# Loading gamma and the value bias inside the first slot, and changing the filters and pointwise weights earlier in it

## The chip, the cores and the metric

The kernel runs on one core of one Trainium2 chip. The metric is the device time of one execution in microseconds (us). A core has five instruction streams that run beside each other and wait for each other through semaphores. TensorE (PE in the profile) multiplies matrices; PEld is its loading of weights. VectorE (DVE) and ScalarE (ACT) do elementwise work, GpSimd (POOL) does elementwise work and issues transfers, and SyncE (SP) only issues transfers. Transfers run on 16 DMA engines. Each stream takes its instructions strictly in the order in which the program wrote them.

## The reference

Two layers act on an array x of 4 pictures of 64 by 64 pixels with 256 channels.

Layer 0 is full self-attention in each picture (4096 tokens, queries and keys of 32 channels), scaled by one number gamma and added to x:

```
q = x @ Wq + bq;  k = x @ Wk + bk;  v = x @ Wv + bv
attn = softmax(q k^T)                       # 4096 x 4096 per picture
x = gamma * (attn @ v) + x
```

Layer 1 filters each channel with three 3x3 filters ("perceived", 768 channels), applies two pointwise layers with an exact gelu between them and adds the result to x, and then adds a 3x3 windowed attention of the result:

```
perceived = depthwise_conv3x3(x, w_perc) + b_perc      # 256 -> 768
hid = gelu(perceived @ w_up1 + b_up1)                  # 768 -> 512
h = x + hid @ w_up2 + b_up2                            # 512 -> 256
out = h + local_attention_3x3(h, w_qkv, b_qkv)
```

Everything is float32.

## The kernel before, in words

Tokens are cut into blocks of 512 (eight rows of a picture). There are 8 blocks in each of 4 pictures, so 32 *slots*; a slot does the attention of the 512 queries of one block over the 4096 keys of its picture. A slot runs through 16 *points* (`for point in range(points)`, L1176). At each point the program writes the two score matmuls `energy` for weights that are needed two points later (L374; the exponential on ACT, L383, follows), then eight matmuls `product` of weights with values into the accumulators (L392), then one addition on DVE of the weights to the running denominator (`add_up`, L421, its addition at L433). In the slots from the second on, some points run in a split form (L414, L430, L435). The work of layer 1 on earlier blocks is put between the points as jobs. The exponentials go through a ring of three buffers `p` (L382), the scores through a single buffer `e` (L376), and keys through a ring of two tiles `ka` (L293), each loaded by four transfers from a packed copy in device memory (L219 to L223).

The first slot is special. The queries, keys and values of the first picture are projected during it: a start-up part writes blocks 0 to 2 (L1091 to L1106), and then at each odd point two further projections follow (`early_jobs`, L1121; written at L1246). At the even points SP issues the loads of the keys that are due two pairs of points later (`load_keys`, L1182).

All order is that of the written program: the function runs under a manual schedule, so each engine's stream is the sequence in which the Python code calls it, and semaphores for true dependences are put in by the framework.

What the change touches:

- L1107 to L1112, after the start-up part and ahead of the first slot: `gam` (gamma copied to all 128 partitions) and `gbv` (the value bias, two numbers per partition) are loaded by SP, and DVE makes gbv times gamma and `gam_parts`, gamma times a constant. Both are read first when a slot is finished (`finish`, L495 and L501).
- L1218 to L1224, at the end of point 1 of the first slot: GpSimd issues the loads of the layer-1 filters `wb`, their bias, the 1.5 MB of pointwise weights `wup1`, and its bias.
- L1225 to L1230: at points 5, 6 and 7, DVE runs `clear_tap` (L642), 20 very small instructions each, which recombine the filters so that some taps become zero. At point 5 a copy of the bias stands ahead of it.
- L1231 to L1232: at points 9 to 14, DVE runs `turn_weights` (L674), four instructions each on 512 columns, which apply the same recombination to `wup1`.
- After point 15 DVE sums the denominator across partitions (`partial_sums`, L450, lines L458 and L459), PE folds the partial sums (L477), and DVE scales the result into x (`finish`). The first use of the changed filters and weights is in the third slot (`perceive`) and the fourth (`hidden_part`); in the second slot GpSimd reads the changed `wup1` (L1238 and L1240).

Of the kernel before, what the change touches and what calls it, by code (L numbers as in the profile page):

```python
# [12 lines left out]
ALU = mybir.AluOpType  # L13
# [3 lines left out]
P = 128  # L17
# [16 lines left out]
MULT = 3  # L34
# [5 lines left out]
NG = NT // GRP  # L40
# [9 lines left out]
SPLIT = 4096.0  # L50
# [8 lines left out]
def attention_then_perception_kernel(  # L59
# [19 lines left out]
    nc = tc.nc  # L79
# [17 lines left out]
    def unshifted():  # L97
# [1006 lines left out]
            project_v(2, i)  # L1104
        fetch(4)
        fetch(5)  # L1106
        gam = loaded(gamma.partition_broadcast(P), "gam", [P, 1])  # L1107

        gbv = loaded(b_v.rearrange("o (c p) -> p (o c)", p=P), "gbv")
        nc.vector.tensor_scalar(gbv, gbv, gam[:, 0:1], None, ALU.mult)  # L1110
        gam_parts = pool.tile([P, 1], F32, tag="gam_parts", name="gam_parts")
        nc.vector.tensor_scalar(gam_parts, gam, 1.0 + 1.0 / SPLIT, None, ALU.mult)  # L1112
        wlv = pool.tile([P, CH, C], F32, tag="wlv", name="wlv")
        combine = combine_steps()

# [8 lines left out]
        for slot in range(NSLOT):  # L1124
            b, g = divmod(slot, NBLK)
            if slot >= RING:
                renew(slot)
            k, a = slot - LAG_HID, slot - LAG_ATT

            jobs = [  # L1130
                job(hidden_part, k, 0, 0) + job(local_values, k - 1, 1),
                job(local_denominator, a) + job(hidden_part, k, 0, 1),
                job(hidden_part, k, 1, 0), job(hidden_part, k, 1, 1),
                job(local_product, a, 0), job(local_product, a, 1),
                job(update, k, 0), job(update, k, 1), job(guide, k, 0),
                job(guide, k, 1), job(local_values, k, 0), job(scores, k, 0),
                job(scores, k, 1) + job(local_sum, k - 1), [], job(border, k), [],
            ]
            if slot in (1, 2):
                jobs[0] = [lambda: next(combine)] * 2  # L1140
            nxt = []
            if g == NBLK - 1 and b + 1 < B:
                nxt = [projections(slot + 1 + i) for i in range(NBLK)]
                for i in range(2):
                    fetch(slot + 1 + i)
            if slot == 0:
                nxt = [early_jobs[2 * i : 2 * i + 2] for i in range(NG)]
            conv = perceive(slot - LAG_PERC, mixed) if slot >= LAG_PERC else iter(())
            n_mixed = sum(tap != 0 for _, tap, *_ in mixed)
            n_steps, stepped = n_mixed, 0  # L1150


            share = [2, 4, 8, 6, 4, 1, 7, 3, 6, 3, 4, 2, 2, 1, 1, 0]
            if slot == NSLOT - 1:

                jobs = [
                    job(hidden_part, k, 0, 0) + job(local_values, k - 1, 1),
                    job(local_denominator, a) + job(hidden_part, k, 0, 1),  # L1160
                    job(hidden_part, k, 1, 0), job(hidden_part, k, 1, 1) + job(local_product, a, 0),
                    job(update, k, 0), job(update, k, 1) + job(local_product, a, 1),
                    job(guide, k, 0) + job(local_values, k, 0),
                    job(guide, k, 1) + job(local_values, k, 1),
                    job(scores, k, 0) + job(hidden_part, k + 1, 0, 0),
                    job(scores, k, 1) + job(local_sum, k - 1) + job(hidden_part, k + 1, 0, 1),
                    job(hidden_part, k + 1, 1, 0) + job(local_total, a + 1)
                    + job(local_reciprocal, a + 1),
                    job(hidden_part, k + 1, 1, 1), job(update, k + 1, 0) + job(border, k),
                    job(local_product, a + 1, 0) + job(update, k + 1, 1),  # L1170
                    job(local_product, a + 1, 1) + job(local_values, k + 1, 0),
                    job(local_values, k + 1, 1),
                ]
                conv = chain(conv, perceive(slot - 1, upper))
                n_steps += sum(tap != 0 for _, tap, *_ in upper)
            for point in range(points):  # L1176
                G, half = divmod(point, 2)
                after = slot + (G + 1) // NG, (G + 1) % NG
                if half == 0:
                    ahead = slot + (G + 2) // NG, (G + 2) % NG  # L1180
                    if ahead[0] < NSLOT:
                        load_keys(*ahead)  # L1182
                    if 0 < ahead[0] < NSLOT:
                        load_values(*ahead)
                    if G == NG // 2 and slot + 1 < NSLOT:
                        spread_queries(slot + 1)
                behind = slot + (point + 1) // points, *divmod((point + 1) % points, 2)
                if in_parts(*behind):
                    high_part(*behind)
                if after[0] < NSLOT:  # L1190
                    energy(*after, half)
                soon = slot + (point + 3) // points, *divmod((point + 3) % points, 2)
                if in_parts(*soon):
                    load_forms(*soon)
                for do in jobs[point]:
                    do()
                if slot == NSLOT - 1 and point == NHC + 2 * RING:
                    nc.sync.dma_start(out=wup1[:, :MULT, C:], in_=turned_up)
                product(slot, G, half)

                if point == 0:
                    add_up(slot, 0, 0)
                if point < points - 1:
                    add_up(slot, *divmod(point + 1, 2))
                else:
                    partial_sums(slot)


                if slot < NSLOT - 1:
                    to = sum(share[: point + 1])  # L1210
                else:
                    to = min(n_steps, -(-(point + 1) * n_steps // (points - 2)))
                    if point < 3:
                        to = min(to, n_mixed // MULT)
                while stepped < to:
                    next(conv, None)
                    stepped += 1
                if slot == 0 and point == 1:  # L1218
                    wb = const.tile([P, CH, MULT, TAPS + 1], F32, tag="wb", name="wb")
                    nc.gpsimd.dma_start(out=wb[:, :, :, :TAPS], in_=w_perc)  # L1220
                    bias = loaded(b_perc, "bperc", queue=nc.gpsimd)
                    wperc, bperc = wb[:, :, :, :TAPS], wb[:, :, :, TAPS]
                    wup1 = loaded(w_up1, "wup1", queue=nc.gpsimd)
                    bup1 = loaded(b_up1, "bup1", queue=nc.gpsimd)  # L1224
                if slot == 0 and NG - MULT <= point < NG:  # L1225
                    if point == NG - MULT:
                        scratch = tile_of([P, NB], "rden", "scratch")
                        scratch = scratch[:, : (TAPS + 3) * CH].rearrange("p (j c) -> p j c", c=CH)
                        nc.vector.tensor_copy(bperc, bias)
                    clear_tap(point - NG + MULT)  # L1230
                if slot == 0 and NG < point <= NG + 2 * MULT:  # L1231
                    turn_weights(*divmod(point - NG - 1, 2))  # L1232
                if slot == 0 and point == NG:

                    next(combine)
                    blqk = loaded(b_lqk, "blqk", queue=nc.gpsimd)
                if slot == 1 and point == NG:
                    nc.gpsimd.dma_start(out=turned_up, in_=wup1[:, :MULT, C:])  # L1238
                    wup2 = loaded(w_up2, "wup2", queue=nc.gpsimd)
                    mix_weights(  # L1240
                        *blocks_of(wup1, MULT, C), *(wmix[:, i] for i in range(3))
                    )
                    bup2 = loaded(b_up2, "bup2", queue=nc.gpsimd)
                    nc.gpsimd.dma_start(out=wlv, in_=w_qkv[:, :, 2 * C :])
                    blv = loaded(b_lv.partition_broadcast(P), "blv", [P, C], queue=nc.gpsimd)
                if nxt and half == 1:  # L1246
                    for do in nxt[G]:
                        do()
                    if slot and G + 2 < NBLK:
                        fetch(slot + 1 + G + 2)  # L1250
            for _ in conv:
                pass
            if slot < NSLOT - 1:
                next(finish(slot))
# [466 lines left out]
```

## Time and profile before

| what | value |
|---|---|
| median of 3 runs | 3305.59 us (3302.0 to 3307.45) |
| the profiled execution's own time | 3305.77 us |
| span from its first to its last instruction | 3304.1 us |
| PE busy | 3264.6 us, 99% |
| DVE busy | 2905.2 us, 88% |
| ACT busy | 1349.2 us, 41% |
| POOL busy | 500.7 us, 15% |
| mean granted PE clock | 0.997 |

Busy times are those in which an instruction of the engine is under way. The profile's lines give a start in us from the first instruction, a length, the engine (a q behind it means the sequencer that issues), the line of the kernel, the operation and the names of tiles (out<-in), and in brackets how long the engine sat idle before it and what ended that. A transfer's "time to landing" runs from its issue to its last semaphore update.

### The profile page before, as it was taken

The numbers are of one execution on the slowest core, as the hardware profiler recorded it, in microseconds if no ns is written. First come the engines' busy times: TensorE is split into PE (matmuls) and PEld (weight loads), VectorE is DVE, ScalarE is ACT, GpSimd is POOL, SyncE is SP. The second block draws the span as 40 slices with busy tenths as digits, with TensorE's granted clock in tenths as the row PEclk, the third lists the DMA queues.
The fourth block names the chain that finished last, engine by engine and source line by source line (L and its number), as shares of the span: only waits on it lengthen the run. The fifth ranks groups of instructions, "written<-read, shape, count | busy, mean of one in ns | idle before, by whom it ended". The sixth has DMA issues, their size and how long they took to land.

```text
span 3304.1 us, 35658 instructions
## 1 busy us (share of the span) xinstructions
PE 3264.6 (99%) x11986; PEld 2170.4 (66%) x11986; DVE 2905.2 (88%) x4243; ACT 1349.2 (41%) x1647; POOL 500.7 (15%) x627
## 2 busy tenths in 40 slices
PE   8999999999999999999999999999999999999998
PEld 5556666666666666676666666666666666666655
DVE  4788899888999999987999999998799999999894
ACT  3334444444444444444444444444444444444331
POOL 2200011120111110112001111101210011111121
PEclk9999999999999999999999999999999999999999
DMA  6533333464333433346333333435643333333100
GB/s 207 184 113 108 115 115 117 143 193 139 117 115 122 128 116 114 117 149 209 117 116 117 115 122 121 128 105 174 200 130 103 121 112 115 122 122 121 48 18 27
DMA packets 246910, 410.90 MB, mean 124 GB/s; under 512 B 92272, under 2 KB 93312, under 8 KB 246592
## 3 DMA queue, kind: packets, MB, share of 16 engines
q1 hardware_dynamic: 231632, 370.15, 36.8%
q0 software_dynamic: 7408, 24.95, 1.9%
q10 hardware_dynamic: 7680, 13.44, 1.1%
q8 instruction: 99, 1.62, 0.2%
q14 instruction: 91, 0.75, 0.1%
HBM read 346.92 MB, written 60.69 MB: 123 GB/s over the span
## 4 chain that ended last, share of the span: by engine, by line
PE 92%; DVE 4%; DMA 1%; ACT 1%; issue 1%; SPq 0%; POOL 0%; ACTq 0%; DVEq 0%; POOLq 0%
PE acc L402 30%; PE acc L414 16%; PE e L378 7%; PE dx L762 6%; PE hid_bc L705 5%; PE hid_gf L705 5%; PE hid_de L705 5%; PE lv L925 3%; PE g L858 3%; PE v L325 3%; PE lo L1059 3%; PE s L966 2%; PE hid_a L705 2%; DVE perc L592 2%; PE qk L259 1%; PE hid L737 1%
## 5 line engine op out<-in xcount | busy, mean ns | idle before, releaser
L402 PE MATMUL acc<-p,v 128*128 128x512 f32 x2472 | 1113.5, 593 | 0.2 <-ACT v L339 0.2
L592 DVE SCALAR_TENSOR_TENSOR perc<-xp,wb,perc 128x526 f32<-128x526 f32 (+1 forms) x1356 | 969.1, 773 | 0.1
L383 ACT ACTIVATE p<-e 128x1024 f32<-128x1024 f32 x512 | 524.3, 1024 | 1054.3 <-PE e L378 888.0
L402 PEld LDWEIGHTS acc<-p,v 128*128 128x128 f32 x2472 | 466.8, 190 | 486.8 <-issue 472.5
L433 DVE TENSOR_TENSOR den<-den,p 128x1024 f32<-128x1024 f32 x448 | 564.9, 1261 | 1.0 <-ACT p L383 0.6
L991 POOL TENSOR_TENSOR lp<-lp,near 128x396 f32<-128x396 f32 x60 | 150.8, 2513 | 1965.3 <-ACT lp L986 1965.3
L378 PE MATMUL e<-qa,ka 128*128 128x512 f32 x1024 | 427.9, 499 | 13.0 <-ACT p L383 13.0
L378 PEld LDWEIGHTS e<-qa,ka 128*128 128x128 f32 x1024 | 190.0, 190 | 162.7 <-issue 128.0
L388 ACT ACTIVATE ph<-p 128x1024 fp32r<-128x1024 f32 x203 | 214.4, 1056 | 199.4 <-PE acc L414 130.5
L414 PE MATMUL acc<-ph,v 128*128 128x512 f32 x812 | 264.4, 447 | 0.0
L430 DVE TENSOR_TENSOR pl<-p,ph 128x1024 fp32r<-128x1024 f32 x203 | 253.2, 1247 | 12.1 <-ACT ph L388 12.0
L435 DVE SCALAR_TENSOR_TENSOR pg<-pl,ph 128x1024 fp32r<-128x1024 f32 x203 | 256.7, 1264 | 0.0
L762 PE MATMUL dx<-hid,wup 128*128 128x512 f32 x512 | 229.8, 592 | 0.0
L414 PE MATMUL acc<-pg,vf 128*128 128x512 f32 x812 | 222.0, 395 | 1.1 <-DVE pg L435 1.1
L414 PE MATMUL acc<-pl,vf 128*128 128x512 f32 x812 | 219.6, 392 | 0.0
L414 PEld LDWEIGHTS acc<-ph,v 128*128 128x128 f32 x812 | 148.3, 189 | 51.0 <-issue 26.8
L414 PEld LDWEIGHTS acc<-pg,vf 128*128 128x128 f32 x812 | 152.5, 188 | 37.0 <-DVE pg L435 1.5
L414 PEld LDWEIGHTS acc<-pl,vf 128*128 128x128 f32 x812 | 152.7, 188 | 35.6 <-DVE pl L430 0.4
L598 DVE TENSOR_TENSOR perc<-perc 128x262 f32<-128x262 f32 x360 | 168.0, 481 | 6.3
L1014 POOL TENSOR_TENSOR lsum<-lsum,lp 128x99 f32<-128x99 f32 (+1 forms) x179 | 171.8, 966 | 11.7
L728 ACT ACTIVATE hid<-hid,bup 128x512 f32<-128x512 f32 x120 | 80.1, 715 | 215.8 <-DVE hid L712 215.8
L762 PEld LDWEIGHTS dx<-hid,wup 128*128 128x128 f32 x512 | 96.8, 190 | 98.6 <-issue 93.4
(203 smaller groups left out, 3872.4 us busy)
## 6 DMA issues: line engine op xcount, KB each, us to landing
vf<-packed_f SPq DMA_DIRECT2D x203, 512.0 KB, 4.1
ka<-packed SPq DMA_DIRECT2D x1016, 64.0 KB, 3.0
v<-packed_f SPq DMA_DIRECT2D x203, 256.0 KB, 2.7
v<-packed_v SPq DMA_DIRECT2D x203, 256.0 KB, 2.9
v<-packed_v SPq DMA_DIRECT2D x45, 512.0 KB, 3.5
xp<-in_x SPq DMA_DIRECT2D x30, 528.0 KB, 6.8
xc<-in_x SPq DMA_DIRECT2D x56, 256.0 KB, 3.8
out<-lo SPq DMA_DIRECT2D x56, 256.0 KB, 2.0
```

The source lines that it names most:

```text
L378: nc.tensor.matmul(e[:, i, :], lhsT=keys[s, G][:, bass.ts(2 * half + i, P)].bitcast(F32R), rhs=queries[s].bitcast(F32R), start=True, stop= ...
L383: nc.scalar.activation(p, e, AF.Exp)
L388: nc.scalar.activation(high.bitcast(F32R), weights[s, G, half], AF.Identity, scale=BELOW)
L402: nc.tensor.matmul(accs[s][c], lhsT=v[:, i, bass.ts(c, P)], rhs=p[:, i, :], start=(first and i == 0), stop=(last and i == 1),)
L414: nc.tensor.matmul(accs[s][to + c], lhsT=w[:, i, bass.ts(c, P)].bitcast(F32R), rhs=x[:, i, :].bitcast(F32R), start=(to > 0 and n == 0 and ...
L430: nc.vector.tensor_tensor(low.bitcast(F32R), p, high, ALU.subtract)
L433: nc.vector.tensor_tensor(den, before, p, ALU.add)
L435: nc.vector.scalar_tensor_tensor(gap.bitcast(F32R), low, -SPLIT, high, ALU.mult, ALU.add)
L592: nc.vector.scalar_tensor_tensor(acc, win, wt, acc, ALU.mult, ALU.add)
L705: nc.tensor.matmul(ps[:, n * C : (n + 1) * C], lhsT=w(j), rhs=rows_of(mixes[s, j][:, kind, :]), start=(j == 0), stop=(j == MULT - 1),)
L762: nc.tensor.matmul(ps, lhsT=wup2[:, d, bass.ts(c, P)], rhs=hids[s][:, d, :], start=(d == 0), stop=(d == NHC - 1),)
L1014: nc.gpsimd.tensor_tensor(to, to, near_ws[block, half][:, t_, of, :], ALU.add)
```

## The change

The two loads of gamma and the value bias move from before the first slot to the end of its point 1, behind GpSimd's loads of the layer-1 weights in the text, and stay on SP. Their two DVE instructions move to point 3, ahead of the first `clear_tap`. The three `clear_tap` calls move from points 5, 6, 7 to points 3, 4, 5. The six `turn_weights` calls move from points 9 to 14 to points 6 to 11, so two and three points sooner. No instruction is added or removed.

```diff
@@ -1104,12 +1104,7 @@
             project_v(2, i)
         fetch(4)
         fetch(5)
-        gam = loaded(gamma.partition_broadcast(P), "gam", [P, 1])
-
-        gbv = loaded(b_v.rearrange("o (c p) -> p (o c)", p=P), "gbv")
-        nc.vector.tensor_scalar(gbv, gbv, gam[:, 0:1], None, ALU.mult)
         gam_parts = pool.tile([P, 1], F32, tag="gam_parts", name="gam_parts")
-        nc.vector.tensor_scalar(gam_parts, gam, 1.0 + 1.0 / SPLIT, None, ALU.mult)
         wlv = pool.tile([P, CH, C], F32, tag="wlv", name="wlv")
         combine = combine_steps()
 
@@ -1222,14 +1217,18 @@
                     wperc, bperc = wb[:, :, :, :TAPS], wb[:, :, :, TAPS]
                     wup1 = loaded(w_up1, "wup1", queue=nc.gpsimd)
                     bup1 = loaded(b_up1, "bup1", queue=nc.gpsimd)
-                if slot == 0 and NG - MULT <= point < NG:
-                    if point == NG - MULT:
+                    gam = loaded(gamma.partition_broadcast(P), "gam", [P, 1])
+                    gbv = loaded(b_v.rearrange("o (c p) -> p (o c)", p=P), "gbv")
+                if slot == 0 and MULT <= point < 2 * MULT:
+                    if point == MULT:
+                        nc.vector.tensor_scalar(gbv, gbv, gam[:, 0:1], None, ALU.mult)
+                        nc.vector.tensor_scalar(gam_parts, gam, 1.0 + 1.0 / SPLIT, None, ALU.mult)
                         scratch = tile_of([P, NB], "rden", "scratch")
                         scratch = scratch[:, : (TAPS + 3) * CH].rearrange("p (j c) -> p j c", c=CH)
                         nc.vector.tensor_copy(bperc, bias)
-                    clear_tap(point - NG + MULT)
-                if slot == 0 and NG < point <= NG + 2 * MULT:
-                    turn_weights(*divmod(point - NG - 1, 2))
+                    clear_tap(point - MULT)
+                if slot == 0 and 2 * MULT <= point < 4 * MULT:
+                    turn_weights(*divmod(point - 2 * MULT, 2))
                 if slot == 0 and point == NG:
 
                     next(combine)
```

## The prediction

> **What bounds the kernel now.** I read the page first. PE is busy for 99% of the span and leads the chain, so the change can only move time where PE stands still; and only the first slot is edited. So I read that slot in the timeline, then the waits around each hole of PE, then the transfers behind the first hole. PE has two holes there. In the chain that ended last, start and length in us:
>
> ```profile
> 26.76 2.68 SPq L85
> 29.48 9.74 DMA gbv<-in_b_v
> 39.60 1.14 DVE den L433
> 40.82 1.03 ACT p L383
> 41.90 1.22 PE e L378 x2
> ```
>
> The value bias is issued at 29.48 and lands at 39.2. DVE, in order, stands before its scaling; the first denominator addition is behind it. That addition frees the oldest `p` buffer, ACT's fourth exponential waits for the buffer, and PE waits for that exponential, because it frees the only `e`. The timeline has the same from each engine's side:
>
> ```profile
> 39.31 0.23 DVE L1110 TENSOR_SCALAR gbv<-gbv,gam 128x2 f32<-128x2 f32 x1 [12.78 <-DMA gbv<-in_b_v]
> 40.82 1.02 ACT L383 ACTIVATE p<-e 128x1024 f32<-128x1024 f32 x1 [14.28 <-DVE den L433]
> 41.90 1.22 PE L378 MATMUL e<-qa,ka 128*128 128x512 f32 x2 [8.02 <-ACT p L383]
> ```
>
> PE idles 8.02 us, from 33.88 to 41.90. It also restarts slowly. Stages of the timeline, with PE, PEld, DVE, ACT and POOL busy and then PE's granted clock:
>
> ```profile
> 33.90:41.90 8.00, 0.00 (x1) 0.01 (x1) 2.48 (x4) 1.08 (x2) 0.00 (x0) 0.78 0.48 171
> 41.90:45.30 3.40, 3.40 (x5) 1.83 (x6) 2.32 (x4) 2.12 (x3) 0.00 (x0) 0.51 0.41 145
> 82.60:118.20 35.60, 35.35 (x108) 19.92 (x106) 28.72 (x40) 12.74 (x18) 4.84 (x9) 1.00 0.54 183
> ```
>
> The third row shows the rest of the slot: PE without holes, DVE 81% full. The second hole is at the slot's end. The last `turn_weights` stands ahead of DVE's transpose, and PE's fold waits:
>
> ```profile
> 115.75 3.11 DVE L679 SCALAR_TENSOR_TENSOR wup<-wup,coef 128x512 f32<-128x512 f32 x4
> 118.77 0.70 DVE L458 STREAM_TRANSPOSE turned<-den 128x512 f32<-128x512 f32 x1
> 120.34 0.58 PE L477 MATMUL dps<-parts,fold 128*128 128x16 f32 x2 [2.16 <-DVE parts L459]
> ```
>
> The first hole has a second cause behind the first: the keys of the very matmul that restarts. Issues in narrow windows, KB each and us to landing:
>
> ```profile
> wup<-in_w_up POOLq DMA_DIRECT2D x1, 1536.0 KB, 9.6
> gam<-in_gamma SPq DMA_DIRECT2D x1, 0.5 KB, 11.4
> gbv<-in_b_v SPq DMA_DIRECT2D x1, 1.0 KB, 9.7
> ka<-packed SPq DMA_DIRECT2D x1, 64.0 KB, 9.3
> ka<-packed SPq DMA_DIRECT2D x2, 64.0 KB, 8.6
> ```
>
> The last of the four key transfers is issued at 31.5 and lands at 39.9, only 2.0 us before PE restarts. So taking away the wait for gbv alone would give 2.0 us and not 8.0; the rest depends on how much earlier the keys land.
>
> **What the Trainium skill says.** "DMA: Bandwidth & Descriptors", Queues, rings and completion order: each DMA engine goes round the queues that have work for it, packet by packet, and consumes one ring in order. The trace agrees: gamma's 512 bytes, issued at 26.76, land at 38.1, when GpSimd's 1.5 MB (29.28 to 38.8) are nearly through; the bias and the keys follow in the order of their issue. Same page, Issuing engines are not separate DMA queues: the queues share 16 engines; the window 26.5 to 33.9 has them 100% busy. "TensorE: Matmul & The Clock Gate", What's actually happening: an idle window of about 3.4 us halves the clock, a busy one restores it. Here the clock is about a half for 6.8 us, some 38.4 to 45.2, 3.3 us of it after the restart.
>
> **The change, part by part.**
>
> *The two loads leave their place.* SP issues gam in 2.68 us (26.76 to 29.44) and gbv in 0.50. The four key transfers (30.08 to 31.97) inherit that place and are issued about 3.2 us sooner, from 26.8. Gam's long issue is not its own, I assume: SP was similarly slow (2.24 us) at one of the picture loads before it. So the last key may be issued at 28.7 at best and 31.0 at worst; neither decides, since the ring ahead holds picture loads that land until 32.6. What decides is how fast a transfer directly behind them gets through beside `wup1`. Gamma did just that in the before trace: 128 rows, 8 per DMA engine, landing at 38.1. The keys are 128 rows too, but of 2 KB. Estimate: 38.1, plus 8 rows x 84 ns (a 2 KB packet's length in this trace) = 0.7, gives **38.8**. Lower bound: four small transfers that slip between the weights could land with the filter bias, on GpSimd's queue at 34.3, plus some of the 1.5 MB; about 36.5. Upper bound: they come out only behind the weights, as now: 39.9, less the bias's own rows, 39.6. I take 38.8.
>
> *DVE no longer waits.* It is free at 26.5; the additions run at 26.6 and 27.8 (1.22 us each); ACT's fourth exponential runs as soon as PE has its scores, at 28.6. Both are done before PE finishes the projection at 33.88. PE then needs only the keys and starts at 38.9 instead of 41.9: **3.0 us**. If the keys come at 36.5 or 39.6 it is 5.3 or 2.2.
>
> *Clock.* The idle stretch 35 to 38.4 still halves the clock up to 41.8. Before, 3.3 us after the restart ran at half speed and cost 1.65; now (41.8 - 38.9)/2 = 1.45: **0.2 us**. If PE restarts early enough, by some 36.7, the window may count as busy and the whole 1.65 come back.
>
> *The loads' new place on SP.* At point 1 they stand after these keys and before the packed queries of blocks 4 and 5, four picture loads and the keys of point 2. They delay those by their issue, 1 to 3 us. The packed store waits for DVE's L272 after the projection, about 35.3, so the issue is hidden; the keys of point 2 would be issued near 42 instead of 47.5 and PE wants them near 51.5. If that cover were gone, each us would cost one.
>
> *The scaling at point 3.* Two DVE instructions, 0.23 + 0.15 us, on a DVE that in the before trace is idle from 46.2 to 57.2. Gbv lands behind the keys near 40; DVE comes there near 43: no wait. Queued behind it are the filter change, the split of value block 3, and the additions of points 4 and on. The addition at point 4 is first wanted by the exponential at point 6, near 64.5. From gbv to the end of that addition DVE needs 3.7 + 1.8 + 1.2 us, so gbv could land as late as 57 before PE pays.
>
> *The filter change two points sooner.* Three times 3.7 us (61.43 to 65.1 for the first), the first in the idle stretch, at no cost. The other two come with the additions at points 4 and 5: from 55.6 DVE works 1.2 + 3.7 + 1.2 + 3.7 to 65.4, so L272 of the next queries, ready at 62.9, waits 2.5 us. Only a key load behind it waits, landing near 72 for a matmul at 74.5. The filters landed at 34.2, the bias at 34.3. Cost: zero; without that cover up to 2.5.
>
> *The weight change three points sooner.* Six times 3.1 us at points 6 to 11. With two additions and one value split a pair of points asks 2.4 + 6.2 + 1.8 = 10.4 us of DVE while PE needs 11.25; the before trace ran points 9 to 14 so and PE had no hole. `wup1` landed at 38.8. Cost: zero.
>
> *The slot's end.* Nothing stands between the last addition and the transpose. L458 follows L440 at 115.75 and the partial sums are ready at 117.15, before PE's last product ends at 118.18. The 2.16 us hole goes: **2.16 us**. Then DVE's chain from the fold to L435, 15 us long, leads as before, so PE's slightly better clock there gains nothing (1.10 us of waiting for L435 stay or grow).
>
> *Sum.* 3.0 + 0.2 + 2.16 = 5.4 us. From the profiled execution's 3305.77 (span 3304.1 and 1.7 around it): **3300.4 us**. The median of the runs is 3305.59, 0.2 below the profiled one. Afterwards PE leads without a break, so the gain should reach the end.
>
> **Rivals.**
>
> *The keys stop being a limit.* They get through by about 36.5, or 35. Then 5.4 to 7 us of the hole go, with all or part of the 1.65 of clock, and the end's 2.16: 8 to 11 us, about **3296.5**. For it: 256 KB is little, and the small filter loads passed in 5.6 to 6.3 us. Against it: gamma, in just this place, needed 11.4.
>
> *The keys stay the limit, or the end's hole returns elsewhere.* Keys at 39.6, 2.2 us, with the end giving 0 to 2: 1 to 4 us, **3303**. For it: before, everything on SP's queue came out behind the 1.5 MB. Against the second half: nothing else is due on DVE there.
>
> *Slower: the scaling stalls DVE at point 3.* Gamma and the bias have the longest landing times on SP and now stand behind the keys. To lose, gbv has to land after 57; each us beyond costs one, and a net loss over 6.6 us needs some 57 + 5.4 + 6.6 = 69, 39 us after its issue, against 9.7 now. **3313**. Against it: GpSimd's load ends near 39.
>
> **How the numbers follow.** A measurement of this kernel can tell about 0.2%, 6.6 us; so the forecast is inside that. Forecast (gain 4 to 7, 3299 to 3302): 0.52, of which 0.10 lies beyond 6.6 us with the scatter of runs (3302.0 to 3307.45). First rival 0.26, second 0.18, slower 0.04. Faster 0.26 + 0.10 = 0.36; same 0.42 + 0.18 = 0.60; slower 0.04. The range 3295.5 to 3304.3 leaves out the far ends of the first two rivals and the third.
>
> **What would show it.** Right: PE idle about 5 us before the L378 of point 2, now ended by a transfer of ka landing near 38.8 and not by ACT; first L433 at 26.6; no idle time before L1110's successor beyond what DVE has anyway; L477 without a wait on DVE. Wrong: keys landing before 37 or after 39.7; a wait on gbv that reaches PE; new holes of PE at points 4 to 11, or a hole at L477 that remains.

## The result, and the profile after

| | before | after |
|---|---|---|
| median of 13 runs | 3306.24 us (3301.24 to 3309.28) | 3299.50 us (3295.54 to 3302.27) |
| the profiled execution's own time | 3305.77 us | 3302.27 us |
| its span | 3304.1 us | 3300.5 us |
| PE restarts at point 2 of the first slot | 41.90 | 39.09 |
| the fold at the first slot's end (L477) | 120.34 | 115.24 |
| the first product with `pg` in the second slot (L414), called the milestone below | 135.55 | 130.18 |

The ratio of the runs is 0.998, 95% interval 0.9972 to 0.9989: 6.7 us faster, and the interval allows 3.6 to 9.3 (the two ends of the ratio times 3306.24). The forecast was 3300.4. Below, a run's own time is that of its profiled execution.

The chain that ended last, of the kernel after (start, length, what); these four lines stand where the chain of before had the bias, an addition and an exponential:

```profile
28.52 1.25 SPq L223
30.81 8.08 DMA ka<-packed
39.09 1.07 PE e L378 x2
40.17 4.72 PE acc L402 x8
```

The same in its timeline, with the second hole's place below:

```profile
26.36 1.22 DVE L433 TENSOR_TENSOR den<-p,p 128x1024 f32<-128x1024 f32 x1
39.09 1.07 PE L378 MATMUL e<-qa,ka 128*128 128x512 f32 x2 [4.26 <-DMA ka<-packed]
42.40 0.22 DVE L1224 TENSOR_SCALAR gbv<-gbv,gam 128x2 f32<-128x2 f32 x1
112.38 0.69 DVE L440 TENSOR_TENSOR den<-den 128x512 f32<-128x512 f32 x1
113.18 0.71 DVE L458 STREAM_TRANSPOSE turned<-den 128x512 f32<-128x512 f32 x1
115.24 0.29 PE L477 MATMUL dps<-parts,fold 128*128 128x16 f32 x2
126.28 0.73 PE L378 MATMUL e<-qa,ka 128*128 128x512 f32 x2 [1.98 <-ACT p L383]
```

DVE now begins its additions at 26.36 and not at 39.5. PE still stops at point 2, but what ends the stop is the transfer of the keys. The bias is scaled at 42.40 with no wait in front. At the slot's end the transpose follows the last addition and the fold waits for nobody. The last line is new in size: the second slot's third pair of score matmuls waited 0.56 us before and 1.98 now:

```profile
131.65 0.74 PE L378 MATMUL e<-qa,ka 128*128 128x512 f32 x2 [0.56 <-ACT p L383]
```

This line is from the kernel before. DVE's chain from the fold leads there in both kernels. PE ran at half clock from 120.3 to 123.7 in the kernel before and runs at full clock after the fold now, so it only comes to the wait sooner.

Stages of the kernel after (PE, PEld, DVE, ACT, POOL busy, then PE's clock, DMA share, GB/s):

```profile
33.90:39.10 5.20, 0.94 (x3) 0.09 (x2) 1.83 (x2) 1.26 (x2) 0.00 (x0) 1.00 0.93 292
39.10:42.70 3.60, 3.60 (x6) 1.87 (x7) 1.44 (x5) 1.02 (x1) 0.00 (x0) 0.53 1.18 254
54.00:74.70 20.70, 20.70 (x67) 11.25 (x66) 18.92 (x56) 7.05 (x10) 1.62 (x3) 1.00 0.36 123
2363.70:2367.10 3.40, 3.40 (x5) 1.35 (x4) 3.23 (x7) 0.90 (x1) 0.12 (x1) 0.50 0.73 217
```

The first row is the hole, with the DMA engines 93% busy; the second the restart at half clock. The third holds the filter changes and the first weight changes at their new points: DVE is busy for 18.9 of 20.7 us and PE has no hole. The fourth explains why this one execution shows only 3.5 us at its end. At the milestone it is 5.37 us ahead; near 2365 it loses 1.8 us, 1.7 of them in a window at half clock, which the profiled execution before did not have there:

```profile
2364.00:2370.00 6.00, 3.19 (x12) 1.82 (x11) 2.88 (x5) 2.76 (x4) 1.86 (x3) 1.00 0.53 188
```

That line is from the kernel before. PE stands still there for 2.8 us before and 2.7 after, waiting for an exponential; a halved clock follows in some of the profiled executions and not in others. So the experiments are read at the milestone, to some tenths of a us, and the end times give the total.

### The profile page after: what moved, and what is told of

It reads as the page before. It is cut to its first block, busy times and chain, and to the rows that moved or that the text cites. A ratio compares the mean times of both kernels' runs of the same rounds, so it can differ in the third digit from the quotient of the medians.

```text
span 3300.5 us, 35656 instructions
## 1 busy us (share of the span) xinstructions
PE 3266.1 (99%) x11986; PEld 2170.0 (66%) x11986; DVE 2905.6 (88%) x4243; ACT 1349.2 (41%) x1647; POOL 501.6 (15%) x627
## 4 chain that ended last, share of the span: by engine, by line
PE 85%; DVE 12%; issue 2%; DMA 1%; ACT 1%; POOL 0%; SPq 0%; ACTq 0%; DVEq 0%; POOLq 0%
PE acc L402 28%; PE acc L414 14%; PE e L378 6%; PE dx L762 5%; PE hid_bc L705 5%; DVE perc L592 5%; PE hid_gf L705 4%; PE hid_de L705 4%; PE v L325 3%; PE lv L925 3%; PE g L858 3%; PE lo L1059 2%; PE hid_a L705 2%; PE s L966 2%; DVE den L433 2%
## 5 line engine op out<-in xcount | busy, mean ns | idle before, releaser
L433 DVE TENSOR_TENSOR den<-den,p 128x1024 f32<-128x1024 f32 x448 | 565.2, 1262 | 4.1 <-ACT p L383 3.9
L414 PE MATMUL acc<-ph,v 128*128 128x512 f32 x812 | 264.4, 447 | 0.0
L430 DVE TENSOR_TENSOR pl<-p,ph 128x1024 fp32r<-128x1024 f32 x203 | 253.3, 1248 | 12.1 <-ACT ph L388 12.0
L435 DVE SCALAR_TENSOR_TENSOR pg<-pl,ph 128x1024 fp32r<-128x1024 f32 x203 | 256.9, 1265 | 0.0
L414 PE MATMUL acc<-pg,vf 128*128 128x512 f32 x812 | 222.0, 395 | 1.1 <-DVE pg L435 1.1
L414 PE MATMUL acc<-pl,vf 128*128 128x512 f32 x812 | 219.7, 392 | 0.0
L414 PEld LDWEIGHTS acc<-ph,v 128*128 128x128 f32 x812 | 148.3, 189 | 51.1 <-issue 26.8
L414 PEld LDWEIGHTS acc<-pg,vf 128*128 128x128 f32 x812 | 152.4, 188 | 37.0 <-DVE pg L435 1.5
L414 PEld LDWEIGHTS acc<-pl,vf 128*128 128x128 f32 x812 | 152.7, 188 | 35.6 <-DVE pl L430 0.4
```

The costliest lines, as they stand in the source:

```text
L414: nc.tensor.matmul(accs[s][to + c], lhsT=w[:, i, bass.ts(c, P)].bitcast(F32R), rhs=x[:, i, :].bitcast(F32R), start=(to > 0 and n == 0 and ...
L430: nc.vector.tensor_tensor(low.bitcast(F32R), p, high, ALU.subtract)
L433: nc.vector.tensor_tensor(den, before, p, ALU.add)
L435: nc.vector.scalar_tensor_tensor(gap.bitcast(F32R), low, -SPLIT, high, ALU.mult, ALU.add)
```

## The experiments

**The two halves of the change, each alone.** The first keeps the loads' and the scaling's new place, and puts filter and weight changes back (against the kernel after; `...` marks lines left out):

```diff
-                if slot == 0 and MULT <= point < 2 * MULT:
-                    if point == MULT:
+                if slot == 0 and point == MULT:
                         ... the two scaling instructions
+                if slot == 0 and NG - MULT <= point < NG:
+                    if point == NG - MULT:
                         ...
-                    clear_tap(point - MULT)
-                if slot == 0 and 2 * MULT <= point < 4 * MULT:
-                    turn_weights(*divmod(point - 2 * MULT, 2))
+                    clear_tap(point - NG + MULT)
+                if slot == 0 and NG < point <= NG + 2 * MULT:
+                    turn_weights(*divmod(point - NG - 1, 2))
```

> Only the two loads and their two scaling instructions are moved; filter and weight changes stay at points 5 to 7 and 9 to 14. Theory A (two separate holes: the first ends with the keys' landing, the second is the last weight change standing before the transpose): PE restarts at about 39.1, the fold at L477 keeps its wait of 2.2 us, and the first L414 on pg in the second slot (135.55 before, 130.18 after) starts at 132.7. Rival C (the earlier filter changes are what frees DVE): PE restarts at 41.9 and the first L414 on pg stays at 135.5.

Its timeline:

```profile
39.29 1.19 PE L378 MATMUL e<-qa,ka 128*128 128x512 f32 x2 [4.80 <-DMA ka<-packed]
118.50 0.37 PE L477 MATMUL dps<-parts,fold 128*128 128x16 f32 x2 [2.18 <-DVE parts L459]
```

The first hole is shortened as in the kernel after, the second is as before. The milestone came at 133.50 and not 132.7, because of the clock:

```profile
37.40:44.25 6.85, 4.96 (x7) 2.49 (x8) 1.67 (x4) 1.02 (x1) 0.00 (x0) 0.50 1.07 260
```

Here 5.0 us after the restart ran at half speed, (44.25 - 39.29)/2 = 2.5 us lost, against 3.4/2 = 1.7 in the kernel after, whose halved window lay at 39.2 to 42.64. Own time 3303.44. The filter changes do not free DVE; the loads do.

The second half alone is the same exchange of point numbers in the kernel before, with the loads left in place:

```diff
-                if slot == 0 and NG - MULT <= point < NG:
-                    if point == NG - MULT:
+                if slot == 0 and MULT <= point < 2 * MULT:
+                    if point == MULT:
                         ...
-                    clear_tap(point - NG + MULT)
-                if slot == 0 and NG < point <= NG + 2 * MULT:
-                    turn_weights(*divmod(point - NG - 1, 2))
+                    clear_tap(point - MULT)
+                if slot == 0 and 2 * MULT <= point < 4 * MULT:
+                    turn_weights(*divmod(point - 2 * MULT, 2))
```

> The loads and the scaling stay before the first slot; filter and weight changes move to points 3 to 5 and 6 to 11. Theory A: PE restarts at 41.9 as before, no wait at L477, the first L414 on pg starts at 133.0 (2.2 to 2.6 sooner than 135.55). Rival C: the restart comes forward to 39; a third possibility, that the earlier changes crowd DVE: a new hole of PE between 55 and 80 and the first L414 on pg at 135 or later.

```profile
41.76 1.22 PE L378 MATMUL e<-qa,ka 128*128 128x512 f32 x2 [7.96 <-ACT p L383]
118.13 0.29 PE L477 MATMUL dps<-parts,fold 128*128 128x16 f32 x2
```

The first hole is untouched, the wait at the fold is gone, and the milestone is at 133.06, 2.49 us sooner. No new hole of PE in the slot. Own time 3302.11. With 2.05 for the loads alone (135.55 - 133.50) the two halves make 4.5 of the 5.37; the rest is the 0.8 us of clock just named.

**Which of the changes fills the second hole.** In the kernel after, only `turn_weights` goes back to points 9 to 14:

```diff
-                if slot == 0 and 2 * MULT <= point < 4 * MULT:
-                    turn_weights(*divmod(point - 2 * MULT, 2))
+                if slot == 0 and NG < point <= NG + 2 * MULT:
+                    turn_weights(*divmod(point - NG - 1, 2))
```

> The changed kernel with the weight changes back at points 9 to 14, the filter changes staying at points 3 to 5. If the last weight change is the whole second hole: restart 39.1, the wait of 2.2 us at L477 is back, the first L414 on pg starts at 132.7, as in the run with the loads alone, so the filter changes' new place is worth nothing. If the filter changes had a part in it, the wait at L477 is under 2 us.

```profile
38.96 1.19 PE L378 MATMUL e<-qa,ka 128*128 128x512 f32 x2 [5.14 <-DMA ka<-packed]
117.39 0.58 PE L477 MATMUL dps<-parts,fold 128*128 128x16 f32 x2 [2.18 <-DVE parts L459]
```

The whole wait is back, and the milestone is at 132.61. Own time 3304.63, with a window at half clock near 2368. The weight change is the second hole; the filter change's new place is worth nothing that shows here.

**Taking DVE's wait away without moving the keys forward.** The loads go back to their old place, the scaling stays at point 3:

```diff
         fetch(5)
+        gam = loaded(gamma.partition_broadcast(P), "gam", [P, 1])
+        gbv = loaded(b_v.rearrange("o (c p) -> p (o c)", p=P), "gbv")
         ...
-                    gam = loaded(gamma.partition_broadcast(P), "gam", [P, 1])
-                    gbv = loaded(b_v.rearrange("o (c p) -> p (o c)", p=P), "gbv")
```

> The changed kernel with the loads of gamma and the bias back in their old place ahead of the first slot, the scaling staying at point 3. This takes away DVE's wait alone. The forecast's step says the keys then land at 39.9 as before and PE restarts at 40.0: 1.9 us of the 8 won by the wait and 0.9 less than in the changed kernel, the first L414 on pg at 131.0. If the place on SP's queue is worth nothing, PE restarts at 39.1 as in the changed kernel.

```profile
26.38 1.22 DVE L433 TENSOR_TENSOR den<-p,p 128x1024 f32<-128x1024 f32 x1
40.11 1.19 PE L378 MATMUL e<-qa,ka 128*128 128x512 f32 x2 [6.29 <-DMA ka<-packed]
```

DVE is free 13 us sooner and PE gains 1.8. This is the plainest view of the first hole: two waits that end within 2 us of each other lay side by side, and the profile before names only the one that ended last. The 1.0 us between 40.11 and 39.09 is what the keys' place on SP's queue is worth. The milestone came at 131.92, 0.9 later than expected: again PE ran at half clock for long after the restart, 5.1 us. Own time 3301.35.

**Is it the 1.5 MB that holds the keys up?** The pointwise weights and their bias are loaded at the end of point 4, on the same queue of GpSimd, so that they are issued near 51 and not near 29. First in the kernel after:

```diff
-                    wup1 = loaded(w_up1, "wup1", queue=nc.gpsimd)
-                    bup1 = loaded(b_up1, "bup1", queue=nc.gpsimd)
                     ...
+                if slot == 0 and point == MULT + 1:
+                    wup1 = loaded(w_up1, "wup1", queue=nc.gpsimd)
+                    bup1 = loaded(b_up1, "bup1", queue=nc.gpsimd)
```

> The changed kernel with the 1.5 MB of pointwise weights and their bias loaded at the end of point 4 instead of point 1. Theory A (the 1.5 MB beside them set when the keys land): the last key load lands by 34.8, PE restarts by 35, its clock isn't halved there, and the first L414 on pg starts at about 124.2 to 125; total 6 us below the changed kernel, 3293 to 3294. Theory B (the keys are late for a reason of their own, the queue's order or the packed store that they read): restart stays at 38 to 39.1 and the time at 3299. A third possibility, that the transfer only collides later: a new hole of PE at points 4 to 6, at most 2 us gained.

The last key load and the weights (KB, us to landing), and PE's restart:

```profile
ka<-packed SPq DMA_DIRECT2D x1, 64.0 KB, 3.6
wup<-in_w_up POOLq DMA_DIRECT2D x1, 1536.0 KB, 8.6
```

```profile
34.23 0.70 PE L378 MATMUL e<-qa,ka 128*128 128x512 f32 x2 [0.43 <-DMA ka<-packed]
108.71 0.29 PE L477 MATMUL dps<-parts,fold 128*128 128x16 f32 x2
```

The keys land in 3.6 us (at 34.0) where they took 8.1 in the kernel after. PE's hole is 0.43 us, its clock is not halved there, and no new hole appears in the slot. The milestone is at 123.64. Median 3295.35 us, ratio to before 0.9964 (0.995 to 0.9978): some 4 us below the kernel after, where 6 were expected. The two profiled executions differ by the expected amount, 6.5 us at the milestone (130.18 - 123.64) and 7.3 in their spans (3300.5 and 3293.2, both with a half-clock window near 2360). The medians come from different occasions, and the runs of each kernel spread by some 2 to 3 us each way; set against the kernel before of its own occasion, each is lower by 6.7 (3306.24) and by 11.9 us (3307.28), which makes 5.2 between them.

Then the same move in the kernel before, with nothing else:

> The kernel before with the 1.5 MB loaded at the end of point 4 and nothing else changed. Theory A: the value bias lands near 34.5, DVE's first addition follows at once, PE restarts at about 36.9, 5 us sooner than 41.90, and with part of the clock the time falls by 5 to 6.5 us; the wait at L477 stays. Theory B (the place in SP's queue decides): the bias lands at 38 or later, PE restarts after 40.5, and the time falls by less than 1.5 us.

```profile
33.81 0.23 DVE L1110 TENSOR_SCALAR gbv<-gbv,gam 128x2 f32<-128x2 f32 x1 [7.30 <-DMA gbv<-in_b_v]
36.39 1.12 PE L378 MATMUL e<-qa,ka 128*128 128x512 f32 x2 [2.54 <-ACT p L383]
114.89 0.45 PE L477 MATMUL dps<-parts,fold 128*128 128x16 f32 x2 [2.18 <-DVE parts L459]
```

The bias lands at 33.7, PE restarts at 36.39: 5.5 us sooner; the wait at the fold stays. Median 3299.53, ratio 0.9978 (0.9967 to 0.9989), about what the whole change gave (0.998). One large load, with its small bias, issued later does as much as the change's three moves.

And half of it, in the kernel after: 0.75 MB at point 1, the other half at the end of point 4.

```diff
-                    wup1 = loaded(w_up1, "wup1", queue=nc.gpsimd)
+                    wup1 = const.tile(list(w_up1.shape), F32, tag="wup1", name="wup1")
+                    nc.gpsimd.dma_start(out=wup1[:, :MULT], in_=w_up1[:, :MULT])
                     ...
+                if slot == 0 and point == MULT + 1:
+                    nc.gpsimd.dma_start(out=wup1[:, MULT:], in_=w_up1[:, MULT:])
```

> The changed kernel with the pointwise weights loaded in two halves of 0.75 MB, the first at point 1 as in the changed kernel, the second at the end of point 4. If the keys' landing grows with the bytes beside them (38.9 with 1.5 MB in the changed kernel, 34.0 with none in the run before this one), half of them give 36.4 and PE restarts near 36.5. If the order alone counts, so that the keys come out whenever any bulk load is there, they land near 38.5; if only the last part of the bulk hurts, near 34.5.

```profile
36.84 0.90 PE L378 MATMUL e<-qa,ka 128*128 128x512 f32 x2 [2.79 <-DMA ka<-packed]
```

The last keys land at 36.6. With 0, 0.75 and 1.5 MB beside them that makes 34.0, 36.6 and 38.9: the keys come through about when the bulk does (landed at 36.4 and 38.3). Own time 3297.67, milestone 127.95.

The transfers show how. These are the packets, MB and engine share of GpSimd's queue (q0) and SP's (q1), in the kernel before from 34 to 35 us, then in the kernel after from 33 to 34 and from 37 to 38:

```profile
q0 software_dynamic: 26, 0.32, 76.8%
q1 hardware_dynamic: 26, 0.00, 1.4%
```

```profile
q0 software_dynamic: 28, 0.34, 88.9%
q1 hardware_dynamic: 19, 0.03, 10.2%
```

```profile
q1 hardware_dynamic: 318, 0.26, 81.1%
q0 software_dynamic: 11, 0.01, 4.2%
```

While the bulk runs, the two queues get about one packet each in turn: 26 to 26 in the kernel before, where those of SP hold only some bytes (gamma and the bias come next on its queue), and 28 to 19 in the kernel after. A packet of the bulk holds 12 KB (0.34 MB in 28) and one of SP's under 2 KB (0.03 MB in 19), so SP's queue gets a tenth of the engines' time until the bulk is nearly out. That fits the 11.4 us that gamma's 512 bytes, spread over 128 partitions, took. The halved load has packets of 6 KB, so it halved the bytes and the packets together; 1.5 MB in smaller packets was not tried.

**A version that is better than both.** After the late bulk, PE's remaining holes near the first slot are at the start of the second one, behind DVE's chain from the fold, in which GpSimd's `mix_weights` (L637) runs beside DVE. On top of the late bulk, the mixing is held back until point 8 of the second slot by a copy of one column of a tile that DVE writes there (the transfers of GpSimd behind the copy start later too):

```diff
                 if slot == 1 and point == NG:
+                    held = const.tile([P, 1], F32, tag="held", name="held")
+                    nc.gpsimd.tensor_copy(held, gaps[1, NG // 2, 0][:, 0, 0:1])
                     nc.gpsimd.dma_start(out=turned_up, in_=wup1[:, :MULT, C:])
```

> The kernel with the late 1.5 MB, and GpSimd's mixing of the weights (L637 in the kernel before) held back until point 8 of the second slot by a one-column copy of a tile that DVE writes there. If GpSimd's work beside it is what stretches DVE's scaling of the first slot's result (1.9 us each against a median of 0.75), the pair takes 1.5 us, the chain from the fold to the first L435 shortens by about 4 us, PE's holes of 2.0 and 1.1 us at the second slot's start go, and the time falls by 3 to 3.7 us to about 3292. If those instructions are long for another reason, nothing changes there and the time stays at 3295; if the mixing only stretches DVE elsewhere, PE shows new holes near point 8.

Median 3293.95 us, ratio to before 0.9964 (0.995 to 0.9978). The mechanism was there (fold at 109.95, milestone at 121.15, so 11.2 us between them and not 14.9), but against 3295.35 of another occasion the total was unclear, also because this execution had a window at half clock near 21 us, where no other profile has one. So both once more on one chip:

> The kernel with the late 1.5 MB again, beside the next one on the same chip, since the two were timed on different occasions. Expected: the median 11 to 12 us below the kernel before.

> The kernel with the late 1.5 MB and the held-back mixing again. Its profile showed 3.7 us won at the second slot's start and 0.7 lost to a new hole near point 8, and two windows at half clock that cost 1.7 us each, one of them near 21 us where no other profile has one. If that window is a matter of the single execution, this one is about 3 us below the kernel with the late 1.5 MB on the same chip; if it comes with the edit, they are level.

| | median of 5 | lowest to highest | ratio to before |
|---|---|---|---|
| late bulk | 3295.39 us | 3294.02 to 3296.07 | 0.9965 (0.9951 to 0.9979) |
| late bulk and late mixing | 3293.30 us | 3292.73 to 3293.83 | 0.9960 (0.9947 to 0.9974) |

The five runs of each do not overlap: 2.1 us, a little under the 3 expected. The half-clock window near 21 us did not come again. With the late bulk alone PE also ran at half clock for 3.4 us at the second slot's start (from 120.6, and from 121.4 in the repeat); with the late mixing it did not. DVE's part of the chain, with the late bulk alone:

```profile
111.28 0.74 DVE L495 SCALAR_TENSOR_TENSOR o<-acc,gam_parts,den 128x512 f32<-128x512 f32 x1
111.95 3.87 DVE L501 SCALAR_TENSOR_TENSOR xp<-o,gbv,xp 128x512 f32<-128x512 f32 x2
115.74 0.68 DVE L810 COPY wqk_turned<-wq_turning 128x512 f32<-128x512 f32 x1
118.49 2.83 DVE L430 TENSOR_TENSOR pl<-p,ph 128x1024 fp32r<-128x1024 f32 x1
119.73 0.73 PE L378 MATMUL e<-qa,ka 128*128 128x512 f32 x2 [1.97 <-ACT p L383]
```

and with the late mixing, in its second profile:

```profile
111.93 0.74 DVE L495 SCALAR_TENSOR_TENSOR o<-acc,gam_parts,den 128x512 f32<-128x512 f32 x1
112.60 1.41 DVE L501 SCALAR_TENSOR_TENSOR xp<-o,gbv,xp 128x512 f32<-128x512 f32 x2
113.93 0.68 DVE L810 COPY wqk_turned<-wq_turning 128x512 f32<-128x512 f32 x1
116.26 1.22 DVE L430 TENSOR_TENSOR pl<-p,ph 128x1024 fp32r<-128x1024 f32 x1
120.55 1.09 PE L414 MATMUL acc<-pg,vf 128*128 128x512 f32 x4
149.94 1.20 PE L414 MATMUL acc<-pg,vf 128*128 128x512 f32 x4 [0.68 <-DVE pg L435]
```

Of these instructions, L501 takes 1.41 in place of 3.87 us and L430 1.22 in place of 2.83, and PE no longer waits there; 0.7 us come back as a new wait where the mixing runs now. The Trainium skill's "GPSIMD Engine Reference", Specifications, says that GpSimd shares its access to the on-chip memory with VectorE and contends with VectorE instructions that read two such inputs. L501 and L430 do, and the pair of kernels agrees, with factors of 2.7 and 2.3. L495 and the copy L810 take one input, or their only one, from where PE writes its results, and beside the mixing (111.1 to 120.2) they keep 0.74 and 0.68 us. Where the mixing runs now, 141.3 to 151.6, L433 and L435, which also read two such inputs, take 2.8 to 2.9 us each from 144.3 on. The last of them begins at 149.8, when the two transfers issued ahead of the mixing have landed (148.4), so it is the mixing and not they.

## Why the prediction was right

*The first hole.* The step gave the keys 38.8 and PE 38.9; they landed at 38.9 and PE restarted at 39.09, 2.81 us sooner where 3.0 were forecast. Ahead of the wait PE finished its projection at 34.8 and not at 33.9, which cost nothing, since the keys came later. The estimate took gamma's landing in the trace before as the measure for whatever stands directly behind the picture loads, and added the keys' bytes. The experiments show why that served: what stands there comes out about with the bulk, 38.3 in the kernel after, because its packets take turns with the bulk's large ones. The forecast's first rival, keys at 36.5, is what half of the bulk gives.

*That the wait alone would be worth 2.0 us and not 8.* Shown by the run that took it away alone: 1.8.

*Clock.* Forecast 0.2 us; in this pair the shift is the same 2.8 us at the restart and at the next pair of score matmuls, so nothing. The step took the halved window to stay where it was and to end at 41.8; it lay at 39.2 to 42.6, all of it behind the restart. The run with the loads alone lost 0.8 us more there than the kernel after, at nearly the same restart. That scatter is larger than the term. The hope that a restart by some 36.7 would save the clock was wrong too: in the kernel before with the late bulk PE restarted at 36.39 and ran at half clock from 36.5 to 39.9.

*The loads' new place, and the scaling.* Gamma and the bias landed at 39.1 and 39.3, and DVE came there at 42.40. The keys of point 2 were issued from 40.7, landed at 45.2 and were wanted at 51.9. Hidden, as forecast.

*The earlier filter and weight changes.* DVE reached L272 at 65.69 (forecast 65.4) and PE had no hole. Cost zero, as forecast.

*The slot's end.* Forecast 2.16 us; the shift grows from 2.8 to 5.10 at the fold, which is 2.3. At the milestone it is 5.37, since the fold itself took 0.29 us at full clock and not 0.58; from the fold's end to the milestone it is 14.6 us in both kernels, and in all eight other profiles with the mixing in its old place. The step that said that a better clock gains nothing there was wrong by this 0.3 us: the fold is the one matmul on which DVE's chain hangs.

*Sum.* 5.4 us were forecast and 5.37 are there at the milestone. The two main terms held to 0.2 us each; that the sum fits to some hundredths is luck, since the restart and the clock came out 0.2 short each, and the slot's end and the fold gave 0.1 and 0.3 more. The step "the gain should reach the end" held for the runs as a whole (6.7 us, interval 3.6 to 9.3) and not for this pair of profiled executions, of which the later lost 1.8 near 2365. Whether halved windows there are more likely with this change stays open: they are in the profiles of the kernel after, of the late bulk (twice), of the late mixing (twice) and of the run with the weight changes put back; they are not in those of before, of either half alone, of the late bulk in the kernel before, of the halved bulk and of gamma first. The first list holds only kernels with the loads and the filter changes moved; but the halved bulk, without such a window, has both too.

## What to carry to other kernels

A wait in the profile is named after what ended last. Before taking it away, look up when the next thing that the same instruction needs is ready; if that is only 2 us earlier, 2 us is the whole gain. A large load that is not urgent, issued on another queue, can hold up small urgent loads for as long as it runs: here by 2.6 us for 0.75 MB and 4.9 for 1.5 MB. Issue it behind the first stall that it could lengthen. And at a stage boundary, what stands on an engine ahead of the instruction that hands over to the busiest engine can cost most of its length (here 2.3 us of a weight change of 3.1); move it to where that engine has slack.

## What the runs showed of the hardware that was not expected

- The four key loads, 256 KB, issued from 26.7 to 30.8, got no lead over the 1.5 MB that were issued on another queue at 29.2 and landed at 38.3: the last of them landed at 38.9, and at 34.0 with the 1.5 MB gone. Between the two queues the engines took turns by packets (26 to 26 in one microsecond, 0.32 MB against 0.00) and not by bytes.
- After holes of 4.3, 4.8 and 5.1 us in the same place (kernel after, loads alone, weight changes put back), PE ran at half clock for 3.4, 5.0 and 3.3 us after its restart. The halved windows that were measured around the two holes are 3.4 or 6.8 us long in every profile that has one; what differs is how much of one lies behind the restart, and in the kernel after it began 0.1 us behind it. Shorter holes were followed by a halved clock too: 2.2 us at the fold in all four profiles with that wait. Near 2360 it followed holes of 2.02 (late bulk) and 2.67 us (kernel after), and not those of 2.48 (loads alone) and 2.81 us (kernel before). A difference of 1 to 2 us between two single profiled executions can be this alone.
